# First transfers of a kernel: their order, their division, and their landing times in the planner's account

## The chip, the cores and the metric

One Trainium2 chip, one core. The time is the device time of one execution in microseconds (us), the median of several runs. Engines are named as in the profile: PE (matmul), PEld (its weight loads), DVE (VectorE), ACT (ScalarE), POOL (GpSimd), SP (SyncE; here it only issues transfers). "Lnnn" is a line of the kernel before, unless it is said to be of the changed one.

## The reference, cut to what matters

Eight sequences of 128 tokens with 128 channels (float32) go through eight sublayers, each added to the residual x. The change touches only how the first of them gets its data:

```python
x = x + _L0_xattn_ref(_layernorm(x, axis=-1), ctx_1024, ctx_1024, mask, w_q, b_q, w_k, b_k, w_v, b_v, w_o, b_o)
x = x + _L0_ffn_ref(_layernorm(x, axis=-1), ...)      # soft mixture of slots
x = x + _L1_xattn_ref(_layernorm(x, axis=-1), ctx_1024, ...)
x = x + _L1_ffn_ref(_layernorm(x, axis=-1), ...)      # 64 experts, top 3
...                                                   # L2 and L3: attention, 6 + 2 local layers
```

`_L0_xattn_ref` is a cross attention with 16 heads of 8: queries from the normalised x, keys and values from a context of 77 rows per sequence, with an integer mask of 128 x 77 per sequence, then an output projection. So its keys need w_k, b_k and the context; its values w_v, b_v and the context; its queries x, w_q and b_q; its scores the mask; its output w_o and b_o.

## The kernel before, in words

**Two plans.** The kernel's work is recorded as steps (`plan.add`), each with the engines that may take it and an assumed duration in ns, and then put into an order by a list scheduler (`Plan.arranged`): at each moment of its own account, each engine takes the first recorded step whose inputs have come and for whose tiles there is room. The instructions are then issued in exactly that order, engine by engine. There is one plan for the front (L0 attention, L0 ffn, L1 attention, routing, experts) and another for all later layers. Where two engines may take a step (a copy by ACT or DVE, a spreading of keys by POOL or DVE), the account also decides which does. So an assumed time that changes at the start of the front can move any later step of the front, and the engine that takes it. It can't change the order within the second plan.

**The account's transfers.** A transfer is a step of SP. Its assumed duration blocks SP in the account, and what it writes counts as come a further 2000 ns later (`TAIL`). Before the change the durations grow with size: 540 for two sequences of x, 1000 for the context, 1300 for the pack "wa", 500 for half the masks, 880 for four sequences of x, then 600 (col), 2500 (w0), 3800 (row), 6500 (w1).

**Packs.** Small weights are laid side by side on the host (`Pack`). "wa" holds w_q, w_k, w_v, w_o, a head pattern and four biases of L0's attention: 774 columns, 387 KB. It lies in the tile `wide`, with w0 of the L0 ffn behind it. All of `plan_l0_xattn` is recorded with `plan.also = [come["ctxT"], wav]`: every step of it waits, in the account, for the whole context and all of wa. The built instructions wait only for the transfers that they read.

**The first transfers, on SP's one queue, in this order:** x of sequences 0 and 1 (128 KB), context (308 KB), wa (387 KB), x of 2 and 3 (128 KB), two halves of the masks (154 KB each), x of 4 to 7 (256 KB), col (167 KB), w0 (768 KB), row (1056.5 KB), w1 (2048 KB), cst, wg, eight zero fills of a DRAM table, b2, w, and then expert weights (256 KB each) as tiles come free. As built, from the ninth transfer on each also waits for the transfer eight places before it.

**L0's attention** runs in parts of two, two and four sequences (`some`, L1069). For a part: statistics and normalisation of x (L775, L777 on DVE, L768 to L784 on POOL, L792 on ACT or L794 on DVE), keys (matmul at L761, bias at L1077, spreading over heads at L1081), transposes of the normalised x (L754) and their copy (L741 or L743), queries (L761, bias at L1090), the mask as 0 or -1e30 (L1092). Then for each sequence: values (L761, bias at L924), the mask put into four PSUM banks by a matmul with the identity (L843), scores as 16 small matmuls of 32 rows (L847; the profile has two records for a float32 matmul), exponentials (L855), row sums and outputs as small matmuls of 32 columns (L863), division (L868 to L870), projection (L883, L884), addition to x (L1099).

**The end of the front.** When x is done for the last sequence, its tokens are routed: 24 indirect stores by POOL (L1323), twelve of them behind the last sequences, then reads of the gathered rows by SP (L1381) and the experts (L1421, L1442), whose remaining 90 weight loads stand behind these reads in SP's order.

Of the kernel before, what the change touches and what calls it, by code (L numbers as in the profile page):

```python
# [16 lines left out]
I32 = mybir.dt.int32  # L17
# [7 lines left out]
P = 128  # L25
B = 8
KC = 77
# [38 lines left out]
def gated_bias(b):  # L66

    return padded_rows_halves(b).reshape(6, P).T
# [67 lines left out]
def laid_out(i):  # L136

    i = {k: np.asarray(v) for k, v in i.items()}
    cst = shape_constants()

    row = Pack()
    for name in ("L1_xattn_b_out", "L1_xattn_gate", "L1_ffn_gate_b",
                 "L2_xattn_bv", "L2_xattn_bo", "L2_xattn_g1",
                 "L2_xattn_b1", "L2_xattn_bf2", "L2_xattn_g2", "L2_xattn_b2", "L2_ffn_q_scale",
                 "L2_ffn_k_scale", "L3_ffn_q_scale", "L3_ffn_k_scale"):
        row.add(name, i[name].reshape(1, -1))

# [12 lines left out]
    col.add("L1_ffn_b1", i["L1_ffn_b1"].reshape(NE, 4, P).transpose(2, 0, 1))  # L160

    wa = Pack()
    for name in ("w_q", "w_k", "w_v", "w_o"):
        wa.add("L0_" + name, i["L0_xattn_" + name].T)
    p = np.arange(P)
    wa.add("heads4", (p[:, None] // 8 % 4 == np.arange(4)[None, :]).astype(np.float32))
    for name in ("b_q", "b_k"):
        wa.add("L0_" + name, i["L0_xattn_" + name].reshape(P, 1))
    for name in ("b_v", "b_o"):
        wa.add("L0_" + name, np.broadcast_to(i["L0_xattn_" + name].reshape(1, P), (P, P)))  # L170
# [12 lines left out]
    w = Pack()  # L183
    for n in ("q", "k"):
        w.add(f"L2_W{n}_pair", i["L2_xattn_W" + n][:, np.arange(P) ^ 1])
    for name in ("Wq", "Wk", "Wv", "Wo", "W1"):
        w.add("L2_" + name, i["L2_xattn_" + name])
    w.add("L2_W2", chunked(i["L2_xattn_W2"]))
    w3 = Pack()
    w3.add("L3_q", i["L3_xattn_Wq"])  # L190
    w3.add("L3_kv", i["L3_xattn_Wkv"])
    w3.add("L3_o", chunked(i["L3_xattn_Wo"]))

    def local(m, qkv, wo, a, b):
# [9 lines left out]
    arrays = {  # L204
        "x": i["x"], "mask": i["mask_Bx1xSxS2_if1"].reshape(B, P, KC),
        "maskT": np.ascontiguousarray(i["mask_Bx1xSxS2_if1"].reshape(B, P, KC).transpose(2, 0, 1)),
        "ctxT": np.ascontiguousarray(i["ctx_1024"].reshape(B * KC, P).T),
        "cst": cst.array(), "row": row.array(), "col": col.array(), "wa": wa.array(), "w0": w0.array(), "w1": w1.array(),
        "wg": wg.array(), "w": w.array(), "w3": w3.array(),
        "experts": np.ascontiguousarray(experts), "expert_b2": i["L1_ffn_b2"],  # L210
        "l2a": l2a, "l2b": l2b, "l2o": l2o, "l3a": l3a, "l3b": l3b,
    }
    return arrays, {"cst": cst.at, "row": row.at, "col": col.at, "wa": wa.at, "w0": w0.at, "w1": w1.at, "wg": wg.at,
                    "w": w.at, "w3": w3.at}


# [754 lines left out]
def plan_front(w, early, dram, wide, narrow):  # L971

    c, nc, plan, a = w.c, w.c.nc, w.plan, w.c.a
    c.room("w1", early)

    places = Context.places(plan, wide, narrow)
    n = [a[name].shape[1] for name in ("wa", "w0")]
    c.packs["wa"], c.packs["w0"] = wide[:, 0 : n[0]], wide[:, n[0] : n[0] + n[1]]
    wav, w0v = (plan.part(places[0], lambda t: t) for _ in range(2))
    come = {}  # L980

    def load(name, ns, emit, vals=None):
        come[name] = plan.fixed(None)
        plan.add({"SP": ns}, emit, [], [come[name], *(vals or [])])

    def pack(name, ns):
        load(name, ns, lambda e: c.load(name))

    def x_in(b0, n):
        load("x", 200 + 170 * n, lambda e: nc.sync.dma_start(c.x[:, b0 : b0 + n, :], a["x"][b0 : b0 + n].rearrange("b s d -> s b d")),  # L990
             w.xs[b0 : b0 + n])

    x_in(0, 2)
    load("ctxT", 1000, lambda e: nc.sync.dma_start(c.ctxT, a["ctxT"]))
    plan.add({"SP": 1300}, lambda e: c.load("wa"), [], [wav])
    x_in(2, 2)
    masks = [w.tile([P, 4, KC] if w.general else [KC, 4, P], I32) for _ in range(2)]

    def mask_half(h):
        at = slice(4 * h, 4 * h + 4)  # L1000
        nc.sync.dma_start(masks[h](), a["mask"][at].rearrange("b s k -> s b k") if w.general else a["maskT"][:, at, :])
# [5 lines left out]
    plan.add({"SP": 2500}, lambda e: c.load("w0"), [], [w0v])  # L1007
    pack("row", 3800)
    pack("w1", 6500)
    pack("cst", 3000)  # L1010
# [1 line left out]
    route = Routed(w, early, dram, come)  # L1012
# [25 lines left out]
    plan.also = [w0v, come["col"]]  # L1038
    l0f = plan_l0_ffn(w)
    for part in parts:  # L1040
        l0f(*part)
# [11 lines left out]
            route.some(*then[i])  # L1053
            plan.also = also
    plan.also = [come["col"]]
    route.experts(Context(w, places, (wav, w0v), vzs))
    plan.also = []
    return route


def plan_l0_xattn(w, masks, narrow):
    c, nc, plan = w.c, w.c.nc, w.plan
    wa = lambda name: c.get("wa", name)
# [5 lines left out]
    def some(b0, n):  # L1069
        xs = w.xs[b0 : b0 + n]  # L1070
        xh, xT, qT = w.tile([P, n, P]), w.tile([P, n, P]), w.tile([P, n, P])
        w.normed(lambda k: xh()[:, k, :], lambda k: xs[k](), xs, [xh], n=n)
        mask, fills = masks[b0 // 4], plan.fixed(fill[:, b0 : b0 + n, :])
        ps, kT, kb = w.bank([P, n, KC]), w.tile([P, n, KC]), w.tile([P, n, 4, KC])
        w.mm(lambda: ps().rearrange("p b k -> p (b k)"), lambda: wa("L0_w_k"),
# [3 lines left out]
        def apart(e):  # L1079
# [11 lines left out]
            qT(), qs(), wa("L0_b_q"), float(1.0 / np.sqrt(8.0)), ALU.add, ALU.mult), [qs], [qT])  # L1091
        plan.add({"DVE": 100 + 75 * n}, lambda e: nc.vector.tensor_scalar(  # L1092
            fills(), mask()[:, b0 % 4 : b0 % 4 + n], 0.0, -1e30, ALU.is_equal, ALU.mult), [mask], [fills])
        for j in range(n):
            b, x = b0 + j, xs[j]
            vz = vzs[b % 4]
            w.values_8(b, wa("L0_w_v"), wa("L0_b_v"), vz)
            out = w.attend_8(qT, j, kb, vz, j, wa("L0_w_o"), wa("L0_b_o"), (fills, spread(fill[:, b, :], 4, 1)))
# [1099 lines left out]
```

## Time and profile before

| what | us |
|---|---|
| median of 3 runs | 1552.71 (1550.05 to 1555.53) |
| the profiled execution | 1561.18 |
| its span, first to last instruction | 1559.4 |
| PE busy (share of the span) | 1425.1 (91%) |
| ACT, DVE, POOL busy | 936.9, 920.4, 816.6 |
| mean granted PE clock | 0.952 |

The profiled execution is 8.5 us slower than the median of the others, so a difference is worked out within it and then carried over to the median.

The start of the span, from the timeline of all engines (start and duration in us, engine, line, operation, out<-in, count, and in brackets the idle time before it and what ended it):

```profile
0.72 0.45 SPq L990 DMA_DIRECT2D x_res<-in_x_dram  x1
1.23 0.46 SPq L994 DMA_DIRECT2D ctxT_sb<-in_ctxT_dram  x1
...
1.74 0.42 SPq L256 DMA_DIRECT2D wide<-in_wa_dram  x1
2.21 0.43 SPq L990 DMA_DIRECT2D x_res<-in_x_dram  x1
...
2.95 0.49 DVE L775 BATCH_NORM_STATS2 few<-x_res 128x6 f32<-128x128 f32 x2 [2.95 <-DMA x_res<-in_x_dram]
```

Each issue takes SP about 0.43 us. The first x is issued at 0.72 and DVE starts on it at 2.95.

### The profile page before, as it was taken

How to read it: one execution, taken by the hardware profiler on the slowest of the kernel's cores; microseconds unless marked ns; L12 is line 12 of the kernel's file. 1: busy time of each engine (PE TensorE's matmuls, PEld its weight loads, DVE VectorE, ACT ScalarE, POOL GpSimd, SP SyncE). 2: the span in 40 equal slices, each digit the busy share in tenths (PEclk: the TensorE clock that was granted, in tenths of full speed). 3: DMA queues.
4: the chain of work that ended last, by engine and by line, in shares of the span. 5: the costliest groups of instructions: out<-in, count | busy, mean ns of one | idle time of the engine just before them, and what ended most of it. 6: DMA issues, size and time to landing. Idle time of an engine off the chain costs nothing.

```text
span 1559.4 us, 39024 instructions
## 1 busy us (share of the span) xinstructions
PE 1425.1 (91%) x16007; PEld 972.3 (62%) x16007; DVE 920.4 (59%) x1995; ACT 936.9 (60%) x1917; POOL 816.6 (52%) x1243
## 2 busy tenths in 40 slices
PE   7999998598587869999999999999999999899996
PEld 4777775375363555675666766667666667475654
DVE  5543764523356428668577585766857665657563
ACT  3676564253245846666666666666666676566764
POOL 3310225310566727777595674956749572536561
PEclk7999999699697989999999999999999999999997
DMA  9300001388301000100100010010000000000000
GB/s 335 131 1 21 8 2 42 111 296 324 124 21 69 1 1 1 56 16 2 42 16 15 2 56 16 1 49 23 2 22 22 2 22 2 21 2 1 1 2 16
DMA packets 39964, 74.00 MB, mean 47 GB/s; under 512 B 4102, under 2 KB 18630, under 8 KB 38496
## 3 DMA queue, kind: packets, MB, share of 16 engines
q1 hardware_dynamic: 33888, 66.16, 12.3%
q0 software_dynamic: 1536, 3.15, 0.6%
q8 instruction: 128, 2.10, 0.5%
q10 hardware_dynamic: 4352, 2.10, 0.5%
q14 instruction: 60, 0.49, 0.1%
HBM read 65.10 MB, written 6.29 MB: 46 GB/s over the span
## 4 chain that ended last, share of the span: by engine, by line
PE 59%; DVE 19%; ACT 8%; POOL 7%; issue 4%; DMA 2%; another core or an unknown queue 0%; ACTq 0%; SPq 0%; POOLq 0%; DVEq 0%
PE mm L1757 8%; PE mm L754 7%; PE mm L761 5%; PE mm L1843 5%; DVE big L1779 4%; DVE big L1781 4%; DVE few L1783 4%; PE mm L1868 3%; PE mm L1929 3%; PE mm L1984 3%; PE mm L1961 2%; PE mm L1974 2%; PE mm L863 2%; PE mm L1189 2%; PE mm L1175 2%
## 5 line engine op out<-in xcount | busy, mean ns | idle before, releaser
L741 ACT COPY big<-mm 128x512 f32<-128x512 f32 (+4 forms) x512 | 276.4, 565 | 222.0 <-PE mm L754 118.0
L1784 POOL TENSOR_TENSOR big<-big,big 128x512 f32<-128x512 f32 x224 | 283.8, 1275 | 237.1 <-DVE big L1781 232.0
L1757 PE MATMUL mm<-wide,big 128*128 128x512 f32 x672 | 323.5, 611 | 13.1 <-ACT big L741 10.6
L1797 POOL TENSOR_TENSOR big<-big,few 128x512 f32<-128x512 f32 x224 | 226.8, 1042 | 1.6
L754 PE MATMUL mm<-ident,big 128*128 128x128 f32 (+1 forms) x1430 | 206.4, 280 | 19.5 <-ACT big L792 4.4
L754 PEld LDWEIGHTS mm<-ident,big 128*128 128x128 f32 (+1 forms) x1430 | 162.7, 143 | 96.8 <-POOL big L1797 31.9
L1757 PEld LDWEIGHTS mm<-wide,big 128*128 128x128 f32 x672 | 120.0, 194 | 116.3 <-issue 83.9
L1779 DVE TENSOR_TENSOR big<-mm,big 128x512 f32<-128x512 f32 x224 | 152.4, 680 | 64.0 <-ACT big L1778 61.0
L1778 ACT ACTIVATE big<-mm 128x512 f32<-128x512 f32 x224 | 133.0, 597 | 91.0 <-PE mm L1757 83.5
L1781 DVE TENSOR_TENSOR big<-mm,big 128x512 f32<-128x512 f32 x224 | 152.4, 680 | 5.3 <-ACT big L1778 5.3
L1783 DVE TENSOR_REDUCE few<-big 128x8 f32<-128x512 f32 x224 | 151.0, 674 | 6.5 <-ACT big L1778 6.5
L1875 ACT ACTIVATE big<-mm 128x512 f32<-128x512 f32 x224 | 118.2, 610 | 34.4 <-PE mm L1868 34.4
L1843 PE MATMUL mm<-narrow,big 128*128 128x128 f32 x896 | 117.2, 283 | 11.6 <-DVE big L1891 11.3
L1843 PEld LDWEIGHTS mm<-narrow,big 128*128 128x128 f32 x896 | 108.6, 196 | 28.3 <-DVE big L1891 17.9
L1885 DVE TENSOR_TENSOR mm<-mm,big 128x512 f32<-128x512 f32 x64 | 44.5, 696 | 132.0 <-ACT big L1884 130.5
L1929 PEld LDWEIGHTS mm<-big,big 128*32 128x32 f32 x3072 | 86.7, 110 | 27.9 <-issue 27.2
L1868 PE MATMUL mm<-big,big 64*64 64x64 f32 (+2 forms) x3584 | 100.4, 238 | 1.2 <-ACT big L741 1.2
L1868 PEld LDWEIGHTS mm<-big,big 64*64 64x64 f32 x3584 | 94.2, 133 | 6.3 <-ACT big L741 2.0
L1929 PE MATMUL mm<-big,big 128*32 128x128 f32 x3072 | 94.1, 273 | 0.1
L822 POOL TENSOR_TENSOR big<-big,tiny 128x308 f32<-128x308 f32 x40 | 27.9, 700 | 97.3 <-DVE tiny L819 47.2
L1891 DVE SCALAR_TENSOR_TENSOR big<-mm,big 128x512 f32<-128x512 f32 x112 | 73.1, 686 | 5.6 <-PE mm L1929 0.4
L743 DVE COPY big<-mm 77x512 f32<-77x512 f32 (+2 forms) x74 | 47.6, 656 | 29.7 <-PE mm L1189 9.1
(277 smaller groups left out, 2335.4 us busy)
## 6 DMA issues: line engine op xcount, KB each, us to landing
big<-in_experts_dram SPq DMA_DIRECT2D x128, 256.0 KB, 4.9
wide<-in_l2a_dram SPq DMA_DIRECT2D x6, 1536.0 KB, 6.6
narrow<-in_l2b_dram SPq DMA_DIRECT2D x6, 534.0 KB, 3.5
narrow<-in_l2o_dram SPq DMA_DIRECT2D x6, 512.0 KB, 3.6
p_w<-in_w_dram SPq DMA_DIRECT2D x1, 2048.0 KB
expert_rows<-big SPq DMA_DIRECT2D x8, 256.0 KB, 13.9
big<-expert_rows SPq DMA_DIRECT2D x8, 256.0 KB, 3.8
expert_ys<-big ACTq DMA_DIRECT2D x16, 128.0 KB, 4.3
```

Source lines behind the costliest of these rows:

```text
L741: nc.scalar.copy(out(), in_())
L754: nc.tensor.transpose(tp()[:, k, :], v(k), c.ident)
L1757: self.plan.add({"PE": 860}, lambda e: nc.tensor.matmul(ps(), lhsT=hs()[:, j, :], rhs=wqkv()[:, o : o + 512], start=True, stop=True), [hs, ...
L1778: yield lambda e: nc.scalar.activation(sq(), heads(), AF.Square)
L1779: yield lambda e: nc.vector.tensor_tensor(t1(), heads(), spread(rot()[:, 2 * kind, :], 8, 1), ALU.mult)
L1781: yield lambda e: nc.vector.tensor_tensor(halves(t2()), halves(heads())[:, :, ::-1, :], sin(), ALU.mult)
L1783: yield lambda e: nc.vector.tensor_reduce(ss()[:, lo : lo + 8], sq(), AX.X, ALU.add)
L1784: yield lambda e: nc.gpsimd.tensor_tensor(t1(), t1(), t2(), ALU.add)
L1797: plan.add({"POOL": 1062}, lambda e, t=t, t1=t1, i=i: nc.gpsimd.tensor_tensor(t(), t1(), spread(r()[:, 8 * i : 8 * i + 8], 64, 2), ALU.mul ...
L1843: nc.tensor.matmul(out(), lhsT=oT()[:, k, :], rhs=wo()[:, 4 * g + k, :], start=(g == 0 and k == 0), stop=(4 * g + k == nch - 1))
L1868: nc.tensor.matmul(sc[s]()[at : at + 64, k, q:end], lhsT=kT()[lo : lo + 64, k, at : at + 64], rhs=qT()[lo : lo + 64, k, q:end], start=Fals ...
L1929: nc.tensor.matmul(avs[half]()[32 * t : 32 * t + 32, k, :], lhsT=vs[t // 2]()[:, at : at + 32], rhs=prs[t]()[:, k, :], start=True, stop=True)
```

## The change

The pack wa is divided in two: "wa" keeps w_q, w_k, b_q, b_k and the head pattern (262 columns, 131 KB), and "wb" gets w_v, w_o, b_v, b_o (512 columns, 256 KB). The context is loaded in two halves of 154 KB. The first transfers are recorded in a new order, and their place in the account is new too: each takes SP 470 ns, and comes by the sum of the bytes recorded so far (3.3 ns per KB, plus 2000 ns, less the time that SP has spent, but at least 2000). The steps of L0's attention wait in the account only for their half of the context and for wa, and from the values on for wb as well; the normalisation waits for x alone.

```diff
+    masks = [...]
+    sent = [0, 0]
+
+    def soon(kb, emit, writes):
+        sent[0] += 470
+        sent[1] += kb
+        plan.add({"SP": 470}, emit, [], writes, tail=max(2000.0, 2000.0 + 3.3 * sent[1] - sent[0]))
+
     def x_in(b0, n):
-        load("x", 200 + 170 * n, lambda e: nc.sync.dma_start(...), w.xs[b0 : b0 + n])
+        soon(64 * n, lambda e: nc.sync.dma_start(...), w.xs[b0 : b0 + n])
+
+    def context(h):
+        come["ctxT", h] = plan.fixed(None)
+        at = slice(4 * h * KC, 4 * (h + 1) * KC)
+        soon(154, lambda e: nc.sync.dma_start(c.ctxT[:, at], a["ctxT"][:, at]), [come["ctxT", h]])
...
     x_in(0, 2)
-    load("ctxT", 1000, lambda e: nc.sync.dma_start(c.ctxT, a["ctxT"]))
-    plan.add({"SP": 1300}, lambda e: c.load("wa"), [], [wav])
+    soon(131, lambda e: c.load("wa"), [vals["wa"]])
+    context(0)
+    mask(0)
+    soon(256, lambda e: c.load("wb"), [vals["wb"]])
     x_in(2, 2)
-    for h in range(2):
-        plan.add({"SP": 500}, lambda e, h=h: mask_half(h), [], [masks[h]])
+    context(1)
     x_in(4, 4)
+    mask(1)
     pack("col", 600)
...
-    plan.also = [come["ctxT"], wav]
-    l0x, vzs = plan_l0_xattn(w, masks, places[1])
+    l0x, vzs = plan_l0_xattn(w, masks, places[1], come, vals["wa"], vals["wb"])
     for part in parts:
         l0x(*part)
-    plan.also = []
+        plan.also = []
...
         w.normed(lambda k: xh()[:, k, :], lambda k: xs[k](), xs, [xh], n=n)
+        plan.also = [come["ctxT", b0 // 4], wav]
...
+        plan.also.append(wbv)
         for j in range(n):
             b, x = b0 + j, xs[j]
             vz = vzs[b % 4]
-            w.values_8(b, wa("L0_w_v"), wa("L0_b_v"), vz)
+            w.values_8(b, wb("L0_w_v"), wb("L0_b_v"), vz)
```

What this makes of the built order of instructions:

- **SP**: x 0-1, wa, context 0-3, mask 0-3, x 2-3, context 4-7, x 4-7, wb, mask 4-7, col, w0, row, w1, and the rest as before. wb is recorded fifth but stands eighth, since it lies in the same tile as wa and waits for it in the account. There are two transfers more and the same bytes. 38 expert weights are issued ahead of the reads of the gathered rows, before and after.
- **PE**, first instructions: keys of part 1, of part 2, of part 3 (this one now waits for the second context half), transposes of part 1, three values (the first waits for wb), queries of part 1, the fourth value, then mask, scores, mask, scores. Before: keys, four values, transposes, queries, transposes of part 2, mask, scores, mask, scores. In the four-sequence part the new order has mask and scores of all four ahead of the row sums and outputs of all four.
- **DVE**: both statistics pairs of part 1 now stand ahead of the first key bias. Before, the second pair's aggregation stood behind it.
- **POOL**: one of the three spreadings of keys (616 columns) is now POOL's, ahead of part 2's normalisation.
- The rest of the front up to the routing is listed anew: PE's listed order differs in places up to its row 1,167 of 7,902 and is the same behind it. DVE takes nine normalisations more (L794) and ACT nine fewer (L792).

More of the change, by code (lines that the diff above doesn't have):

```diff
@@ L162, in laid_out @@
     wa = Pack()
-    for name in ("w_q", "w_k", "w_v", "w_o"):
-        wa.add("L0_" + name, i["L0_xattn_" + name].T)
+    wb = Pack()
     p = np.arange(P)
+    for pack, names in ((wa, "qk"), (wb, "vo")):
+        for n in names:
+            pack.add("L0_w_" + n, i["L0_xattn_w_" + n].T)
+    for n in "qk":
+        wa.add("L0_b_" + n, i["L0_xattn_b_" + n].reshape(P, 1))
+    for n in "vo":
+        wb.add("L0_b_" + n, np.broadcast_to(i["L0_xattn_b_" + n].reshape(1, P), (P, P)))
     wa.add("heads4", (p[:, None] // 8 % 4 == np.arange(4)[None, :]).astype(np.float32))
[L167 to L170, printed above, removed]
     w0 = Pack()
@@ L207, in laid_out @@
         "ctxT": np.ascontiguousarray(i["ctx_1024"].reshape(B * KC, P).T),
-        "cst": cst.array(), "row": row.array(), "col": col.array(), "wa": wa.array(), "w0": w0.array(), "w1": w1.array(),
+        "cst": cst.array(), "row": row.array(), "col": col.array(), "wa": wa.array(), "wb": wb.array(), "w0": w0.array(), "w1": w1.array(),
         "wg": wg.array(), "w": w.array(), "w3": w3.array(),
@@ L212, in laid_out @@
     }
-    return arrays, {"cst": cst.at, "row": row.at, "col": col.at, "wa": wa.at, "w0": w0.at, "w1": w1.at, "wg": wg.at,
+    return arrays, {"cst": cst.at, "row": row.at, "col": col.at, "wa": wa.at, "wb": wb.at, "w0": w0.at, "w1": w1.at, "wg": wg.at,
                     "w": w.at, "w3": w3.at}
@@ L976, in plan_front @@
     places = Context.places(plan, wide, narrow)
-    n = [a[name].shape[1] for name in ("wa", "w0")]
-    c.packs["wa"], c.packs["w0"] = wide[:, 0 : n[0]], wide[:, n[0] : n[0] + n[1]]
-    wav, w0v = (plan.part(places[0], lambda t: t) for _ in range(2))
+    lo, vals = 0, {}
+    for name in ("wa", "wb", "w0"):
+        n = a[name].shape[1]
+        c.packs[name], vals[name] = wide[:, lo : lo + n], plan.part(places[0], lambda t: t)
+        lo += n
     come = {}
@@ L987, in pack, with mask @@
         load(name, ns, lambda e: c.load(name))
-    def x_in(b0, n):
-        load("x", 200 + 170 * n, lambda e: nc.sync.dma_start(c.x[:, b0 : b0 + n, :], a["x"][b0 : b0 + n].rearrange("b s d -> s b d")),
-             w.xs[b0 : b0 + n])
+    masks = [w.tile([P, 4, KC] if w.general else [KC, 4, P], I32) for _ in range(2)]
+    sent = [0, 0]
[3 more added lines that the diff above has]
+        plan.add({"SP": 470}, emit, [], writes, tail=max(2000.0, 2000.0 + 3.3 * sent[1] - sent[0]))
+    def x_in(b0, n):
+        soon(64 * n, lambda e: nc.sync.dma_start(c.x[:, b0 : b0 + n, :], a["x"][b0 : b0 + n].rearrange("b s d -> s b d")),
+              w.xs[b0 : b0 + n])
+    def context(h):
+        come["ctxT", h] = plan.fixed(None)
+        at = slice(4 * h * KC, 4 * (h + 1) * KC)
+        soon(154, lambda e: nc.sync.dma_start(c.ctxT[:, at], a["ctxT"][:, at]), [come["ctxT", h]])
+    def mask(h):
+        at = slice(4 * h, 4 * h + 4)
+        soon(154, lambda e: nc.sync.dma_start(
+            masks[h](), a["mask"][at].rearrange("b s k -> s b k") if w.general else a["maskT"][:, at, :]), [masks[h]])
     x_in(0, 2)
-    load("ctxT", 1000, lambda e: nc.sync.dma_start(c.ctxT, a["ctxT"]))
-    plan.add({"SP": 1300}, lambda e: c.load("wa"), [], [wav])
+    soon(131, lambda e: c.load("wa"), [vals["wa"]])
+    context(0)
+    mask(0)
+    soon(256, lambda e: c.load("wb"), [vals["wb"]])
     x_in(2, 2)
[L997 to L1001, printed above, removed]
-    for h in range(2):
-        plan.add({"SP": 500}, lambda e, h=h: mask_half(h), [], [masks[h]])
+    context(1)
     x_in(4, 4)
+    mask(1)
     pack("col", 600)
-    plan.add({"SP": 2500}, lambda e: c.load("w0"), [], [w0v])
+    plan.add({"SP": 2500}, lambda e: c.load("w0"), [], [vals["w0"]])
     pack("row", 3800)
@@ L1037, in plan_front @@
         plan.add({"DVE": 2500}, lambda e: small_scores(c, (("L2_ffn", 6), ("L3_ffn", 2))), [come["row"]], [])
-    plan.also = [w0v, come["col"]]
+    plan.also = [vals["w0"], come["col"]]
     l0f = plan_l0_ffn(w)
@@ L1055, in plan_front, with plan_l0_xattn @@
     plan.also = [come["col"]]
-    route.experts(Context(w, places, (wav, w0v), vzs))
+    route.experts(Context(w, places, vals.values(), vzs))
     plan.also = []
     return route
-def plan_l0_xattn(w, masks, narrow):
+def plan_l0_xattn(w, masks, narrow, come, wav, wbv):
     c, nc, plan = w.c, w.c.nc, w.plan
-    wa = lambda name: c.get("wa", name)
+    wa, wb = (lambda name, pack=pack: c.get(pack, name) for pack in ("wa", "wb"))
     fill = w.once.tile([P, B, KC] if w.general else [KC, B, P], BF16, name="fill")
@@ L1096, in some @@
             vz = vzs[b % 4]
-            w.values_8(b, wa("L0_w_v"), wa("L0_b_v"), vz)
-            out = w.attend_8(qT, j, kb, vz, j, wa("L0_w_o"), wa("L0_b_o"), (fills, spread(fill[:, b, :], 4, 1)))
+            w.values_8(b, wb("L0_w_v"), wb("L0_b_v"), vz)
+            out = w.attend_8(qT, j, kb, vz, j, wb("L0_w_o"), wb("L0_b_o"), (fills, spread(fill[:, b, :], 4, 1)))
             plan.add({"DVE": 282}, lambda e, x=x, out=out: nc.vector.tensor_tensor(x(), x(), out(), ALU.add), [x, out], [x])
```

## The prediction

> **What bounds the kernel now.** I read the chain of waits first: matmuls hold 59% of it, and from 37 to 249 us of the front PE is never idle for a microsecond. So a start that comes earlier is worth its time only if PE then gets through the same work sooner. The opening is another matter. The waits of the first 17.4 us:
>
> ```profile
> PE mm L761 <- DMA wide<-in_wa_dram: 7.3, 1, 7.3
> POOL tiny L768 <- DVE tiny L777: 5.6, 2, 4.8
> DVE big L1077 <- PE mm L761: 4.7, 1, 4.7
> ...
> PE mm L761 <- ACT big L741: 3.6, 1, 3.6
> ```
>
> Columns: who waited for whom, us in total, times, longest. PE's first matmul waits 7.3 us for the pack wa. The other three lines are one knot, and the timeline unties it:
>
> ```profile
> 7.30 2.39 PE L761 MATMUL mm<-ctxT_sb,wide 128*128 128x154 f32 x6 [7.30 <-DMA wide<-in_wa_dram]
> ...
> 8.19 0.38 DVE L1077 TENSOR_SCALAR big<-mm,wide 128x154 f32<-128x154 f32 x1 [4.75 <-PE mm L761]
> 8.48 0.17 DVE L777 BATCH_NORM_AGGREGATE tiny<-few 128x2 f32<-128x6 f32 x1
> ...
> 9.00 0.64 POOL L768 TENSOR_SCALAR tiny<-tiny 128x2 f32<-128x2 f32 x1 [4.77 <-DVE tiny L777]
> ...
> 11.02 0.88 ACT L792 ACTIVATE big<-x_res,tiny,tiny 128x128 f32<-128x128 f32 x2 [9.01 <-DMA wide<-in_w_dram]
> ```
>
> DVE has its statistics by 3.44, but the key bias L1077 stands in its queue ahead of an aggregation, so normalisation, which needs no weight, waits for the weights' transfer. ACT's line names a DMA; the input that came last is POOL's, at 10.98. A copy then stands behind another normalisation on ACT, the query matmul comes at 15.93, and the first mask matmul (L843) at 17.37. From there PE is full, but slow. Busy time (and count) of PE, PEld, DVE, ACT and POOL by stretch, then PE's granted clock, DMA share, GB/s:
>
> ```profile
> 15.00:20.00 5.00, 4.07 (x24) 2.49 (x28) 3.26 (x12) 1.52 (x4) 2.26 (x4) 0.50 0.96 404
> 20.00:25.00 5.00, 5.00 (x61) 3.12 (x53) 3.97 (x12) 2.42 (x5) 2.22 (x4) 0.50 1.07 332
> 25.00:30.00 5.00, 5.00 (x69) 3.62 (x68) 2.26 (x6) 4.92 (x8) 0.35 (x1) 0.50 0.97 280
> 30.00:35.00 5.00, 5.00 (x43) 3.55 (x42) 0.46 (x2) 1.72 (x5) 0.56 (x2) 0.51 1.01 387
> 35.00:40.00 5.00, 5.00 (x110) 3.88 (x109) 2.71 (x7) 1.15 (x4) 0.91 (x2) 1.00 1.05 386
> ```
>
> In half-microsecond stretches the clock falls at 14.42 and is back at 34.90. A group of L843 takes 1.93 us before and 1.06 behind that point, so the slow stretch costs 45% of its PE time.
>
> **The change, step by step.**
>
> *Transfers.* Summing the GB/s of half-microsecond stretches, the bytes ahead of and including wa (842 kB) have moved by 4.95, and wa lands at 7.16; x 4-7 (1551 kB, 8.0) at 3.53+6.5 = 10.0; col (8.6) at 10.5. So a landing trails its bytes by about 2.1 us; only the very first trailed by 0.5. I take the same bytes at the same rates in the new order: context 0-3 (423 kB, 3.5) lands at 5.6, mask 6.1, x 2-3 6.6, context 4-7 (870 kB) 7.15, x 4-7 8.3, wb (1394 kB, 7.4) 9.5. For the first, 4.0 is the other end (a lag of 0.5), and 6.5 if shorter rows move slower.
>
> Here a rule speaks against the change. The Trainium skill, "DMA: Bandwidth & Descriptors", section "Rules for kernel authors", wants many small transfers coalesced into one large one. Were each of the two added transfers to pay the 2.1 us by itself, keys would start at 7.2 + 4.2 − (842−423 kB at about 290 GB/s = 1.4) = 10.0, later than now. But the seven transfers issued from 0.72 to 3.97 overlap their lags in this trace, so two more cost 2 x 0.43 us of SP, which is early. I take the trace.
>
> *Start of PE.* Keys of parts 1 and 2 at 5.6 (1.16 us, from 7.30 to 8.46). Keys of part 3 wait for the context until 7.2 (1.02). Normalisation is no longer behind L1077: aggregations by 3.9, POOL from 4.3 (its fills end at 4.24), its 1.98 us to 6.3, ACT to 7.2, transposes behind the keys 8.2 to 9.0. Three values wait for wb until 9.5 and take 3 x 0.43; the queries, queued behind them though they need only wa, 10.8 to 12.0; a value to 12.4. DVE reaches the bf16 identity for the mask matmul at about 11.9: key biases 0.37, 0.37, 0.52, fills 2 x 0.28, spreadings 0.77 and 1.42, and statistics, the part-3 pair released by PE at 8.3. POOL's spreading costs about 1.4 us (two rows of half its size at 0.70) and delays only part 2's normalisation, due at 16. So the first mask matmul comes at 12.4 instead of 17.37: 5.0 us. Part 2's transposes (0.6) are now behind it: **4.4 us**.
>
> *The clock.* The trace shows no such start, so it is bounded. All changes of the clock that I looked up lie on a grid of 3.413 us (14.42 + 6, 86, 120 and 139 of them give 34.90, 307.94, 424.02, 488.87). The Trainium skill, "TensorE: Matmul & The Clock Gate", Part 1, has the same free-running window, and says a sustained busy one opens the clock. By that rule the full PE from 17.83 should be fast at 21.25. The trace disagrees: windows filled by mask, scores and L863 stay slow until 34.90. Those that open it hold full-size matmuls: 7.59-11.01 (keys and values, full), 31.49-34.90 (scores 2.0 and full ones 1.4). One with 1.6 us of full ones and 0.5 of mask doesn't. In the new order any window inside 5.6 to 12.4 holds 2.5 to 3.0 us of full matmuls, between the two. If one opens the clock and PE goes straight on, it stays open, as from 35 to 60 with the same mixture. At best the 17.5 us of slow work from 17.37 to 34.90 shrink by 45%, **7.9 us**; at worst the slow stretch runs from 12.4 until the first scores and projections stand together, at about 36, and is 23.6 us long: 6.1 us more, 2.7 us lost. Nearest is the window at 7.59, so I take the best.
>
> *What is late next.* With a fast PE, DVE's queue shows: behind queries and fills it has four score checks (3.9 us, L2001 to L2006), then two divisions with 0.95 us reciprocals each. From the copy of part 2's transposes at about 17, checks, query bias, clamps and reciprocals add up so that part 1's outputs come at about 25, where a fast PE alone would need them at 22. I charge **3.0 us**.
>
> *wb's wait.* Behind the first value on PE stand queries, mask and scores; each us of wb beyond 9.5 delays PE by one, until 15 at no loss against before. *Account and fewer waits* cost no instruction. *Nine normalisations from ACT (0.49) to DVE (0.34)*: 3.1 us of DVE time spread over 230 us in which DVE is about half busy; uncovered, 3.1.
>
> *The order up to the routing.* PE's work is the same; idle PE before 223 is under 2 us, so little can be won. In the tail (223 to 272) it idles about 11 us, between L938, softmaxes and POOL's indirect stores. It could change by −4 to +5; the list ends alike (same stores, divisions, 38 weight loads), so I take 0. From the last store all follows in order: gathered rows at 299.57, 90 weight loads behind them on SP, then the unchanged plan; what the routing gains is kept.
>
> Sum: 4.4 + 7.9 − 3.0 = **9.3 us**. From 1561.18 that leaves 1551.9; carried to the median, 1552.71 − 9.3 = 1543.4.
>
> **Rivals.**
>
> *A: the clock opens late in this phase.* If the new start isn't dense enough but scores of sequence 2 with part 2's transposes open it at 21, the work left up to part 1's projections is two pairs of L863 (4.0), mask and scores (2.1), queries, value and projections (2.0), fast: it ends at about 30. Before, it ends at 34.90 + 2.4 (one L863 pair, value and projection, less transposes done early) = 37.3. So 7 us, **1545.7**. For: such a window (2.0 scores, 0.45 full, 0.95 L863) opened it at 424.02. Against: phase decides.
>
> *B: it opens only at about 36.* Then 4.4 − 2.7 = 1.7 us, **1551.0**. For: scores and masks kept it closed for 17 us. Same result if the transfers land late, for example wb at 13.
>
> *C, slower: the tail is listed worse.* One more group of L949 and projection (1.0 + 1.1) with about 2.5 us of key and query matmuls now stands behind the last block of L938. If that block, which lost 7 us between 246 and 254 to issue gaps beside POOL's stores, loses them again and the added 4.6 no longer fits the tail's idle time (4.1 us from 260 to 280), routing is 4.6 later; with a division pushed behind POOL's twelve stores (15.2 us) a few more. It decides once it exceeds B's gain: 1.7 − 4.6 − 4 = −6.9: **1559.6**. Against: one division fewer stands behind the stores, not more.
>
> *D: it doesn't reach PE.* If keys still started at 7.3, normalisation would still gain 4 us, so this falls into B.
>
> **How the numbers follow.** Forecast (about 9 us) 0.50, A 0.17, B 0.22, C 0.11. A measurement here can tell about 0.3%, 4.7 us, from nothing. Forecast: with ±3 us for the relisting 0.90 of it is faster; A 0.75, B 0.15 (0.75 same, 0.1 slower), C all slower. Faster 0.45 + 0.13 + 0.03, and a little for a slow stretch that is longer in other runs of the old kernel: 0.64. Slower 0.11 + 0.02 = 0.13; same 0.23. Low end: 9.3 + 3 from uncharged DVE delay + 3 from the tail: 1537. High end: B and a little of C, 1554.
>
> **What would show it.** Right: first L761 at 5 to 6.5, first L843 at 12 to 13, clock at 1.00 before 15 and kept through 40, gathered rows near 290. Wrong: PE waiting for wb beyond 11 (transfers), half clock from 15 to 30 (A, B), or L843 early and rows at 299 (C). The forecast fails most easily by the clock.

## The result, and the profile after

| | median (us) | runs | range |
|---|---|---|---|
| before, on the same chip | 1560.57 | 20 | 1550.05 to 1567.24 |
| after | 1551.45 | 20 | 1540.53 to 1558.87 |
| ratio | 0.9944 | | 95% interval 0.9924 to 0.9964 |

The ratio is worth 8.7 us (5.6 to 11.9). The kernel before was itself 7.9 us slower here than in the three runs shown ahead of the prediction; both kernels spread over 17 to 18 us from one execution to the next. The profiled execution of the changed kernel took 1547.99 us (span 1546.1, mean clock 0.958), 13.2 less than that of before.

In the changed kernel's profile line numbers have moved: L756, L763, L845, L849, L865 are L754, L761, L843, L847, L863 of before; L940 is L938, L1096 is L1077, L1343 is L1323, L1401 is L1381.

Waits of the first 17.4 us of after (who for whom, us in total, times, longest):

```profile
PE mm L763 <- DMA ctxT_sb<-in_ctxT_dram: 6.3, 2, 5.1
...
ACT big L794 <- POOL tiny L786: 5.6, 2, 3.8
...
DVE big L1096 <- PE mm L763: 3.2, 2, 2.4
```

PE first waits for the context, no longer for wa; ACT waits for POOL's part of the normalisation and not behind it for anything else; VectorE's longest wait for the keys is 2.4 us instead of 4.7. The knot is undone, as the timeline of all engines shows (start, duration, engine, line, and the wait before it):

```profile
3.27 0.30 DVE L779 BATCH_NORM_AGGREGATE tiny<-few 128x2 f32<-128x6 f32 x2
4.33 0.19 POOL L770 TENSOR_SCALAR tiny<-tiny 128x2 f32<-128x2 f32 x1
...
5.12 1.37 PE L763 MATMUL mm<-ctxT_sb,wide 128*128 128x154 f32 x4 [5.12 <-DMA ctxT_sb<-in_ctxT_dram]
...
5.83 0.88 ACT L794 ACTIVATE big<-x_res,tiny,tiny 128x128 f32<-128x128 f32 x2 [3.82 <-POOL tiny L786]
...
9.57 1.56 PE L763 MATMUL mm<-wide,ctxT_sb 128*77 128x128 f32 x6
...
10.92 0.68 PE L763 MATMUL mm<-big,wide 128*128 128x256 f32 x2
...
11.66 1.03 PE L845 MATMUL mm<-fill,identb 77*77 77x512 bf16 x4
```

Both aggregations stand together at 3.27, normalisation runs at 5.83 instead of 11.02, and the first four mask records come at 11.66 instead of 17.37, in 1.03 us instead of 1.91. The stretches of after (busy time of PE, PEld, DVE, ACT, POOL, then granted clock, DMA share, GB/s):

```profile
15.00:20.00 5.00, 5.00 (x142) 4.22 (x138) 4.17 (x13) 4.98 (x10) 2.33 (x4) 1.00 0.98 408
20.00:25.00 5.00, 4.72 (x75) 3.20 (x68) 4.66 (x14) 3.04 (x6) 1.82 (x4) 1.00 1.07 349
25.00:30.00 5.00, 4.99 (x140) 4.20 (x142) 3.66 (x12) 2.54 (x6) 1.36 (x5) 1.00 1.09 301
30.00:35.00 5.00, 5.00 (x74) 3.72 (x66) 4.62 (x14) 0.00 (x0) 1.81 (x4) 1.00 0.99 374
```

The column to read is the clock, 1.00 where before had 0.50, but with one caution: in every profile here it starts at 1.00 and shows the granted clock only from its first recorded change on, and in after that is a fall at 260. Ahead of it the durations tell: a group of four mask records of 1.03 to 1.06 us is fast, one of 1.91 to 1.93 slow. In after all groups from 11.66 to 40 us are fast (one spans 1.20).

What is left of it at the end of the front, from SP's timeline, before and then after (reads of the gathered rows; second load of the last layers' weights l2a):

```profile
299.57 5.25 SPq L1381 DMA_DIRECT2D big<-expert_rows  x8
...
470.61 0.33 SPq L1717 DMA_DIRECT2D wide<-in_l2a_dram  x1
```

```profile
282.28 5.05 SPq L1401 DMA_DIRECT2D big<-expert_rows  x8
...
456.47 0.33 SPq L1737 DMA_DIRECT2D wide<-in_l2a_dram  x1
```

17.3 us are gained at the rows, 14.1 at l2a, 13.3 at the end. So the profile shows more than the sum of the prediction, and half as much again as the medians. The experiments had to settle which of the two parts of the change gains, by which mechanism, and why executions differ so.

### The profile page after: what moved, and what is told of

The parts are those of the page before. It is cut to its first block, busy times and chain, and to the rows that moved or that the text cites. A ratio compares the mean times of both kernels' runs of the same rounds, so it can differ in the third digit from the quotient of the medians.

```text
span 1546.1 us, 39059 instructions
## 1 busy us (share of the span) xinstructions
PE 1416.7 (92%) x16007; PEld 966.6 (63%) x16007; DVE 922.9 (60%) x2008; ACT 932.3 (60%) x1903; POOL 817.9 (53%) x1244
## 4 chain that ended last, share of the span: by engine, by line
PE 58%; DVE 19%; POOL 9%; ACT 7%; issue 4%; DMA 2%; SPq 0%; POOLq 0%; DVEq 0%; ACTq 0%
PE mm L1777 8%; PE mm L756 7%; PE mm L763 5%; PE mm L1863 5%; DVE big L1799 4%; DVE big L1801 4%; DVE few L1803 4%; PE mm L1888 3%; PE mm L1949 3%; PE mm L2004 3%; PE mm L1981 2%; PE mm L1994 2%; PE mm L1209 2%; PE mm L1195 2%; POOL big L1817 2%
## 5 line engine op out<-in xcount | busy, mean ns | idle before, releaser
L743 ACT COPY big<-mm 128x512 f32<-128x512 f32 (+4 forms) x503 | 272.6, 568 | 218.3 <-PE mm L756 116.7
L1777 PE MATMUL mm<-wide,big 128*128 128x512 f32 x672 | 323.7, 611 | 13.2 <-ACT big L743 10.6
L756 PE MATMUL mm<-ident,big 128*128 128x128 f32 (+1 forms) x1430 | 205.3, 280 | 23.6 <-DVE big L745 4.4
L756 PEld LDWEIGHTS mm<-ident,big 128*128 128x128 f32 (+1 forms) x1430 | 162.2, 143 | 99.9 <-POOL big L1817 32.6
L745 DVE COPY big<-mm 128x512 f32<-128x512 f32 (+3 forms) x83 | 51.2, 635 | 29.5 <-PE mm L1209 7.2
## 6 DMA issues: line engine op xcount, KB each, us to landing
p_w<-in_w_dram SPq DMA_DIRECT2D x1, 2048.0 KB, 13.6
```

Source lines behind the costliest of these rows:

```text
L743: nc.scalar.copy(out(), in_())
L756: nc.tensor.transpose(tp()[:, k, :], v(k), c.ident)
L1777: self.plan.add({"PE": 860}, lambda e: nc.tensor.matmul(ps(), lhsT=hs()[:, j, :], rhs=wqkv()[:, o : o + 512], start=True, stop=True), [hs, ...
```

## The experiments

The table is the key to all of them: for each profiled execution, where PE's clock became fast and stayed so, the first indirect store, start and length of the block of 128 small matmuls (L938, or its line in the other kernel) in the middle of the stores, the reads of the gathered rows, the second load of l2a, and the span. All in us.

| kernel | clock fast from | first store | block at, long | rows | l2a | span |
|---|---|---|---|---|---|---|
| before, first profile | 34.9 | 236.4 | 246.0, 11.0 | 299.6 | 470.6 | 1559.4 |
| e1, before again | 25 | 231.2 | 240.7, 11.1 | 296.3 | 474.1 | 1563.4 |
| e9, before, third | 32.8 | 235.0 | 244.5, 2.5 | 296.1 | 474.2 | 1564.2 |
| e3, new transfers alone | 25 to 28 | 232.9 | 242.5, 10.9 | 297.8 | 470.5 | 1558.3 |
| e5, before, busy start | by 16 | 227.6 | 237.2, 2.5 | 288.1 | 460.6 | 1551.4 |
| after, first profile | 11 | 225.7 | 232.4, 2.4 | 282.3 | 456.5 | 1546.1 |
| e2, after again | 13.9 | 227.7 | 234.4, 13.1 | 292.6 | 468.7 | 1556.6 |
| e8, after, third | 10 | 225.8 | 232.5, 2.4 | 282.4 | 458.1 | 1547.4 |
| e10, after, fourth | 11.8 | 225.8 | 232.5, 2.4 | 282.9 | 454.8 | 1542.9 |
| e4, new list alone | by 10.6; slow again 48 to 58 | 230.9 | 237.6, 13.1 | 297.4 | 472.2 | 1562.0 |
| e6, after, busy start | by 11; slow again 50 to 57 | 229.3 | 236.0, 2.4 | 286.0 | 457.8 | 1545.5 |
| e7, new list alone, busy start | 33.9 (fast to 13.2, then slow) | 233.4 | 240.1, 2.4 | 289.9 | 459.3 | 1547.0 |

What comes behind the l2a column takes 1088 to 1091 us in all twelve: everything that differs, differs before it.

**Theory 1** was that the list (the account of landing times) makes the gain, by an earlier mask part and a clock that is open ahead of it, and that the divided and reordered transfers by themselves gain nothing. The rival was that the transfers gain, by bringing the keys' data earlier.

### Each kernel again (e1, e2)

No edit: the kernel before and the kernel after under new names.

> The kernel before, profiled a second time. Every theory: ratio 1.00 within 0.3%. Theory 1 (the opening's slow clock is a property of its order): PE idles between the key/value matmuls and the query matmul again, the first mask matmul (L843) comes at 17 to 17.5 us and the granted clock is 0.50 for at least 14 us after it. Theory 2 (the slow stretch and the 7 us of issue gaps at 246 us were accidents of one execution): no slow stretch of more than 7 us before 60 us, no gaps. Of the gaps alone I expect that they may or may not return; if they do not, about 6 of the 17.3 us by which the gathered rows came earlier in the changed kernel's profile are not the change's.

> The changed kernel, profiled a second time. Theory 1: ratio to the kernel before 0.992 to 0.997; first mask matmul at 11.5 to 12.5 us, clock 1.00 from before 15 us on and kept. Rival (the clock opens in some executions only): half clock at some time between 15 and 30 us in this profile, with the gathered rows read later than in the first profile of this kernel (282.3 us) by 5 us or more.

Measured, with 75 runs of before beside them (median 1562.9): e1 1565.59, ratio 1.0027 (1.0012 to 1.0041); e2 1557.78, ratio 0.9964 (0.9946 to 0.9983). An unchanged kernel under another name thus came out 0.27% off; differences of that size between two kernels of this case are not to be built on. Against e1 instead of the 75 runs, e2's ratio is 0.9950. In e1 the clock was open ten us earlier than in the first profile of before, without any edit (about 9 us of half speed behind the first mask matmul, where at least 14 were expected), and its first matmul began at 5.70 instead of 7.30. Both of the prediction's starting points were late cases of what an execution of the old kernel does.

### The two halves of the change (e3, e4)

e3 has the new transfers in their new order, with the old assumed times:

```diff
-    load("ctxT", 1000, lambda e: nc.sync.dma_start(c.ctxT, a["ctxT"]))
-    plan.add({"SP": 1300}, lambda e: c.load("wa"), [], [wav])
-    x_in(2, 2)
...
+    load("ctxT", 1000, lambda e: (c.load("wa"), ctx_of(0)))
+    plan.add({"SP": 1300}, lambda e: mask_half(0), [], [wav])
+    x_in(2, 2, lambda e: x_of(2, 2))
...
-    for h in range(2):
-        plan.add({"SP": 500}, lambda e, h=h: mask_half(h), [], [masks[h]])
-    x_in(4, 4)
+    plan.add({"SP": 500}, lambda e: ctx_of(1), [], [masks[0]])
+    plan.add({"SP": 500}, lambda e: x_of(4, 4), [], [masks[1]])
+    x_in(4, 4, lambda e: (c.load("wb"), mask_half(1)))
```

> The divided and reordered transfers of the changed kernel, with the order of every other instruction as before (the account is left as it was). Theory 1 (what counts is the order of the instructions, above all the normalisation no longer standing behind the keys, and a PE without a pause): keys at about 5.1 us, but values wait for wb until 9.6, and the query matmul still stands behind ACT's second normalisation: first mask matmul at 16.5 to 18 us, half clock afterwards, ratio 0.998 to 1.003. Rival (the earlier landing of the keys' data is the gain): ratio 0.993 to 0.996, first mask matmul at 15 us or before.

e4 has the new account, and so the new list, with the old transfers in their old order; wa and wb come in one piece:

```diff
-    soon(131, lambda e: c.load("wa"), [vals["wa"]])
-    context(0)
-    mask(0)
-    soon(256, lambda e: c.load("wb"), [vals["wb"]])
...
+    soon(131, lambda e: nc.sync.dma_start(c.ctxT, a["ctxT"]), [vals["wa"]])
+    soon(154, lambda e: c.load("wab"), [come["ctxT", 0]])
+    soon(154, lambda e: x_of(2, 2), [masks[0]])
+    soon(256, lambda e: None, [vals["wb"]])
...
```

> The changed kernel's order of instructions, with the transfers in one piece and in the order of before. Theory 1: keys at 7.3 us as before, then PE without a pause through keys, transposes, values and queries, so that a window of full matmuls opens the clock in every execution; first mask matmul at 12.5 to 14 us, clock 1.00 from before 16 us on; ratio 0.991 to 0.997, as good as the whole change within 0.2%. Rival (the earlier landing is the gain): first mask matmul at 15 us or later, ratio 0.998 to 1.001.

Measured: e3 1563.32, ratio 1.0004 (0.9986 to 1.0022). e4 1559.62, ratio 0.9969 (0.9952 to 0.9986), level with the whole change in the same comparison (0.9964). PE's timeline of e3:

```profile
5.44 1.37 PE L763 MATMUL mm<-ctxT_sb,wide 128*128 128x154 f32 x4 [5.44 <-DMA ctxT_sb<-in_ctxT_dram]
...
16.12 1.22 PE L763 MATMUL mm<-big,wide 128*128 128x256 f32 x2 [4.11 <-ACT big L743]
...
17.56 1.91 PE L845 MATMUL mm<-fill,identb 77*77 77x512 bf16 x4
```

The keys come at 5.44, and nothing follows from it: the queries still wait 4.11 us for a copy that stands behind another normalisation on ACT, and the mask starts at 17.56, slow. And of e4:

```profile
5.65 2.39 PE L763 MATMUL mm<-ctxT_sb,wide 128*128 128x154 f32 x6 [5.65 <-DMA wide<-in_wab_dram]
...
9.54 1.02 PE L763 MATMUL mm<-big,wide 128*128 128x256 f32 x2
...
10.62 0.81 PE L845 MATMUL mm<-fill,identb 77*77 77x512 bf16 x3
```

With the undivided pack the mask is reached at 10.62, no later than with the divided one, since no value waits for wb. So the gain is the list's, and this settles the first question for Theory 1. The divided transfers bring the keys from between 5.6 and 7.3 (undivided: 7.30, 5.70, 6.12, 5.65) to between 4.9 and 5.4 (divided: 4.90 to 5.12 in four profiles of after, 5.44 in e3), and wb's later landing takes up to 1.0 us of it back.

### The clock by itself (e5), and a start that is busier still (e6, e7, e8)

e5 is the kernel before with matmuls on a tile of ones ahead of part 1's keys (16), transposes (9) and queries (17), in banks that are overwritten next. e6 is the kernel after, e7 the kernel e4, with 9 and 3 of them ahead of the keys of parts 1 and 3. e8 is the kernel after again.

```diff
+    def warm(out, n):
+        for _ in range(n):
+            nc.tensor.matmul(out, lhsT=c.ones, rhs=c.ones, start=True, stop=True)
...
+            keep(flat[:, 0:P], {0: 9, 2: 0, 4: 3}[b0])
+            nc.tensor.matmul(flat, lhsT=wa("L0_w_k"), rhs=c.ctxT[:, b0 * KC : (b0 + n) * KC], start=True, stop=True)
```

> The kernel before, with nothing moved: 16 extra 128x128 f32 matmuls on a tile of ones stand ahead of part 1's first keys, 9 ahead of its transposes and 17 ahead of its queries, each written into the PSUM bank that the step fills next, so that TensorE is busy from about 5 us on. Theory 1 (a large part of the gain is the clock that opens before the mask part): the mask matmuls take 1.03 to 1.06 us a row of four from the first on, at about 16 to 18 us, instead of 1.9; in the two profiles of this kernel the slow stretch ran from 15.8 to about 25 us in one and from 17.4 to 34.9 in the other, at half speed 4.6 to 8.8 us, less up to 3 us that VectorE's queue takes back, so 3 to 5 us less than before: ratio 0.997 to 0.998. Theory 2 (the gain of the list is its order, with the queries no longer behind a wait of 3.5 us; the clock is covered by VectorE): 0 to 1 us, ratio 0.9995 to 1.0005, and VectorE shows longer stretches of busy time between 16 and 40 us.

> The kernel after, with 9 extra 128x128 f32 matmuls on ones ahead of part 1's keys and 3 ahead of part 3's keys. Theory 1: the clock opened at about 10.5 and 13 us in the two profiles of after without them, in some executions surely later; with them it is open at the first keys or before the mask part in all, worth 0.5 to 1 us where it opened early anyway and up to 3 where not: 1 us below after on the mean (range 0 to 2.5), ratio to before about 0.995. Theory 2: no difference from after within 1 us, since what follows waits for VectorE. Slower than after by more than 1 us would mean that the extra work delays the keys.

> The new account and list with the old undivided transfers, as in the run with the list alone, and the same 9 and 3 extra matmuls. If the divided transfers add nothing but an earlier stretch of busy TensorE, this is level with the run above within 1 us (ratio about 0.996). If they bring the keys and values forward in a way that lasts to the end, this stays 1 to 2 us behind it.

> The kernel after once more, beside the three above on one chip, so that they have their own base. From the two comparisons so far (0.9944 and 0.9964): 0.9955, between 0.994 and 0.997. In its profile the clock opens before 14 us; the gathered rows start between 282 and 293 us as in the other two, by where the clock closes after 239 us.

Measured, beside 33 runs of before (1560.48):

| | median | runs | ratio (95%) |
|---|---|---|---|
| e5 | 1558.28 | 22 | 0.9985 (0.9968 to 1.0002) |
| e6 | 1549.75 | 6 | 0.9914 (0.9885 to 0.9943) |
| e7 | 1550.15 | 12 | 0.9925 (0.9900 to 0.9950) |
| e8 | 1547.09 | 6 | 0.9907 (0.9878 to 0.9937) |

PE's timeline of e5 shows the old order with a fast clock (L1106 and L1099 are its queries and transposes):

```profile
15.46 0.60 PE L1106 MATMUL mm<-big,wide 128*128 128x256 f32 x2
15.90 0.38 PE L1099 MATMUL mm<-ident,big 128*128 128x128 f32 x2
16.12 1.03 PE L843 MATMUL mm<-fill,identb 77*77 77x512 bf16 x4
```

The mask part begins where it did in e9 (16.07) and its first store comes at 227.6 instead of 235.0: **7.3 us for the clock alone** up to that store, with nothing moved, in one execution of each (the two ran on different chips). In the new list the same difference can be read between e7 (slow from 13.2 to 33.9) and e8: 233.4 against 225.8, 7.5 us.

The medians show less of it, 2.3 us with an interval that holds zero, and between what the two theories expected. Two things would account for a part: in other executions of the old kernel the clock opens earlier by itself (e1, e3), and later stretches of slow clock give some of it back (e7 is 7.5 us behind e8 at the rows and 1.3 at l2a). But e5 and e8 were measured together and both start with a fast clock, and still their medians are 11.2 us apart, where their profiles are 4.0 apart; e5's profiled execution is among its fastest (1553.24, median 1558.28). So the profiles show what the clock is worth at the front of one execution. How the gain of the medians divides between the clock and the order of the list is not shown.

In e7 the start was filled and the clock closed all the same. PE reached the mask at 9.50 and then waited for VectorE:

```profile
9.50 1.04 PE L845 MATMUL mm<-fill,identb 77*77 77x512 bf16 x3
12.13 0.38 PE L845 MATMUL mm<-fill,identb 77*77 77x512 bf16 x1 [1.59 <-DVE big L1114]
```

The 3.41 us up to the change at 13.2 (one step of the prediction's grid of clock changes) hold only 1.75 us of PE's work.

e8 came out lower than it was expected to (0.9955, no lower than 0.994), which the next section takes up. e6, e7 and e8 don't differ beyond their intervals: filling the start further gains nothing that these runs can tell, and in e6 the clock, open ahead of the first mask matmul, closed again at 50. The undivided transfers under the new list (e7) are again level with the divided ones. None of the versions tried here beat the changed kernel.

### Why the ratios differ: the block between the stores (e9 to e12)

The changed kernel's ratio was 0.9944, 0.9964 and 0.9907 in three comparisons. In all four profiles of the comparison that gave 0.9964 the block of 128 small matmuls took 11 to 13 us, as in the first profile of before; in none of the four of the comparison that gave 0.9907. PE's timeline of e2, part of it:

```profile
234.43 0.94 PE L940 MATMUL mm<-big,big 64*64 64x77 f32 x41
236.38 0.35 PE L940 MATMUL mm<-big,big 64*64 64x77 f32 x4 [1.01 <-issue]
237.80 0.36 PE L940 MATMUL mm<-big,big 64*64 64x77 f32 x3 [1.07 <-issue]
...
244.91 2.63 PE L940 MATMUL mm<-big,big 64*64 64x77 f32 x70 [0.42 <-issue]
```

and of after, with the same instructions in the same order:

```profile
232.41 2.44 PE L940 MATMUL mm<-big,big 64*64 64x77 f32 x128
```

In e2 PE gets through 41 records, then through one to four at a time, idle in between with nothing that the profile could name, until 244.91. POOL's last indirect store of this group runs from 241.89 to 242.85, so the full pace comes back 2.06 us behind its end. In the other four stalled profiles it does so 2.05 to 2.15 us behind it (before: 253.71, last store until 251.56), so the end of the stall goes with the end of the stores. In e2 the clock also closes, from 239.1 to 249. The DMA view of 226 to 246 lists two instruction queues in after:

```profile
q0 software_dynamic: 384, 0.79, 11.5%
q8 instruction: 1, 0.02, 0.3%
q14 instruction: 2, 0.02, 0.3%
```

(packets, MB, share), and in e2 the stores' queue alone:

```profile
q0 software_dynamic: 384, 0.79, 11.4%
```

That would fit an instruction stream that isn't refilled while the stores move. Not every stalled profile bears it out, though. In e4 both queues are silent during the stall as well, but in before, e1 and e3 each moves one packet in it. The DMA view of before, 246 to 253.7, lists among others:

```profile
q8 instruction: 1, 0.02, 0.8%
q14 instruction: 1, 0.01, 0.4%
```

So the missing packets are not what the five stalls have in common. To test whether the stores cause them, e11 and e12 are the kernels before and after without the indirect stores (the experts then read zeros); e9 and e10 are both kernels again, as their base.

```diff
-                def put(e, j=j, k=k):
-                    ...
-                    put = nc.gpsimd.indirect_dma_start(
-                        out=self.rows[:, :], out_offset=bass.IndirectOffsetOnAxis(ap=dsti[:, j, k : k + 1], axis=0),
-                        in_=xh()[:, j, :], in_offset=None)
+                def put(e):
+                    pass
```

> The kernel before once more, as the base of this chip: ratio 1.000, within 0.997 to 1.003. Its profile says whether this chip stalls TensorE in the block of 128 small matmuls that follows the first indirect stores: in six of ten profiles so far the block took 9 to 13 us instead of 2.4, with TensorE idle and waiting for nothing that the profile shows. With the stall the gathered rows are loaded 53 to 56 us after the block's start, without it about 51.

> The kernel after once more. Theory 1 (the block begins about 10 us earlier in every execution, and the stall, where it comes, costs this list about 9 us and the old list about 4): ratio 0.996 to 0.997 if this chip stalls in both profiles, 0.991 to 0.993 if it stalls in neither; in between if the executions are mixed. Block start 232 to 235 us, against 240 to 246 in before. Theory 2 (the ratios of the three comparisons differ by chance alone): 0.994 to 0.995 whatever the stall.

> The kernel before without its indirect stores of the chosen rows: the experts then compute on the zeros that the start writes; every other instruction stays, in the same order. Theory 1 (the stall comes from those stores: [...]the packets of the instruction queues are missing from the trace as long as the stall lasts): the block of 128 small matmuls takes 2.4 to 2.5 us with no idle row in it, also if the kernel before stalls on this chip, and the rows are loaded 5 us earlier or more, as the wait for the stores goes too. Rival (the stall belongs to TensorE's own instruction stream at that place): the block takes 9 us or more here too, whenever it does in the run of before.

> The kernel after without the same stores. Theory 1: no stall, the block takes 2.4 to 2.5 us and begins at 231 to 235 us, about 10 us ahead of the run above; what the change is worth with no stall in either is then 8 to 12 us between this run and the one above, a ratio of the two of 0.992 to 0.995. Rival: the block is as long as in the run of after on this chip.

Measured, beside 35 runs of before (1560.16): e9 1561.91, ratio 1.0006 (0.9983 to 1.0029); e10 1548.55, 0.9932 (0.9912 to 0.9953); e11 1551.56, 0.9941 (0.9916 to 0.9966); e12 1537.97 in four runs, 0.9855 (0.9812 to 0.9899).

By the table five of the ten profiles before these four had stalled, not six, as e9's expectation counts. Neither e9 nor e10 stalls (2.5 and 2.4 us), so that the unstalled blocks of e11 and e12 (2.4 us each, at 244.5 and 241.9) say nothing about the stores: **on the cause of the stall this test is inconclusive**, and it stays open. What did come out is close to what e10's expectation said for no stall, a ratio between 0.991 and 0.993. With the stall the change was worth 0.36%, without it 0.68% and 0.93%, and 0.56% where the first profile of before stalled and that of after did not. Only e2's and e8's intervals lie apart; that of e10 holds the 0.994 of the rival too. Each of the three later comparisons also ran on a chip of its own, one execution of each kernel was profiled in it, and against e1 the 0.36% are 0.50%. So this is an ordering that fits, not a proof. The rows of the table say by how much: from the first store to the rows it is 63.2 to 65.1 us with the stall in the old list and 60.5 and 61.1 without; in the new list 64.8 and 66.5 with it, 56.6 to 57.1 without.

The medians of e12 and e11 lie 13.6 us apart, more than the 8 to 12 expected. But e12 gave one more answer. Its block came at 241.9, not at 231 to 235: the clock did not open at the start. PE's timeline of e12:

```profile
11.28 0.63 PE L763 MATMUL mm<-wide,ctxT_sb 128*77 128x128 f32 x2
11.71 1.91 PE L845 MATMUL mm<-fill,identb 77*77 77x512 bf16 x4
13.55 2.01 PE L849 MATMUL mm<-big,huge 32*77 32x128 f32 x32
```

In this execution the clock became fast at about 35 only. That is the prediction's rival B, in one of the five profiles of the new list with the new transfers and no added matmuls. e11's clock opened at 33.5, so the two show what the list does at a slow clock: the block comes 2.6 us earlier, the first read of the gathered rows 3.9 (262.2 against 266.1). The l2a load, however, comes 13.1 us earlier (454.8 against 468.0). What makes the other nine us between the rows and l2a is open. Changes of the clock on the grid of 3.413 us, counted back from the first recorded one, give the windows of the start; PE's busy time in them, in e10 and then in e12:

```profile
8.35:11.76 3.41, 3.09 (x14) 2.41 (x12) 2.38 (x5) 0.37 (x1) 3.16 (x5) 1.00 1.04 386
```

```profile
8.36:11.78 3.42, 2.81 (x12) 2.42 (x12) 2.54 (x5) 0.37 (x1) 3.17 (x5) 1.00 1.00 371
```

With 3.09 us of 3.41 the clock opened at the window's end, with 2.81 it didn't. The other profiles fit: after with 3.35 and e8 with 3.18 opened, e2 with 2.40 (PE waited 1.0 us for wb in it) opened a window later. Two windows of the old list, worked out in the same way, fit too: 2.9 in e9 and 3.4 in e11 opened. So for full-size matmuls the turning point of these profiles lies between 2.8 and 2.9 us of 3.41, and 0.3 us of PE work in one window decide over 7 us.

## Why the prediction was right

The forecast (9.3 us, 1543.4 from the base then known) stands against 8.7 us (5.6 to 11.9) measured; the time, 1551.45, lies in the range, 8 us above the forecast because the base was 7.9 us higher. That the two gains are so close is partly luck: the later comparisons gave 5.6, 14.5 and 10.6 us, and two terms erred in opposite directions, the clock, worked out from the latest opening seen with the old list, and the tail, put at nothing where it is 4 us shorter without the stall. By its own steps:

- **Transfers.** Keys were put at 5.6 with 4.0 as the other end: 5.12, and 4.90 to 5.09 in four other profiles. wb was put at 9.5: PE begins the values at 9.57, and at 9.47, 9.14 and 9.07 where the wait shows. The working by which each added transfer pays its own lag, with the keys at 10.0, was rightly set aside for the overlapping lags. The rule behind it hardly bears on this case: the Trainium skill, "DMA: Bandwidth & Descriptors", section "Rules for kernel authors", calls transfers under 64 KB mostly overhead, and the divided ones here have 131 to 256 KB; no run has smaller ones in their place. The step overrated what the transfers matter: the 7.3 us of the old profile were a late case, and e3 and e4 show that the transfers gain nothing by themselves.
- **Start of PE, 4.4 us.** First mask matmul at 11.66 instead of the predicted 12.4. With e5 and e10, both at a fast clock, it is 16.12 against 11.76, 4.4.
- **The clock, 7.9 us at best.** The best case came in four of the five profiles of the new list with the new transfers: 7.3 (e5 against e9) and 7.5 (e8 against e7) at the first store. That the clock then stays open, if PE goes straight on, is not refuted: it closed in e4, e6 and e7, with gaps of 1.2 to 1.6 us. "Between the two" was the right reading of a window with 2.5 to 3.0 us of full-size matmuls: it opened with 3.09 and stayed shut with 2.81. The rule of a sustained busy window in the Trainium skill, "TensorE: Matmul & The Clock Gate", Part 1, was rightly not taken alone for the old start: e9's PE is busy from 16.07 on without a gap and its clock opens at 32.8. For the new start, where the busy window holds full-size matmuls, rule and trace agree.
- **What is late next, 3.0 us.** The size was near, the place was not. At a fast clock the mask starts 4.4 us earlier and the first store only 1.8 (227.6 against 225.8), so 2.6 were lost. But PE doesn't wait for VectorE's checks of part 1: between 12 and 35 us of after it idles for 0.3 us. The waits are late, in the part that was said to have little in it either way ("idle PE before 223 is under 2 us"). From the waits of after up to 226 us:

```profile
PE mm L756 <- DVE tiny L821: 1.3, 1, 1.3
PE mm L756 <- POOL big L824: 1.2, 2, 1.1
PE mm L1307 <- POOL before L1300: 0.7, 1, 0.7
```

  The first two, at 160 to 211 us, are reciprocals and divisions of softmaxes that the transposes wait for. e5 has neither; from the first mask matmul to the first store PE idles 1.85 us in it, and 5.05 in after. This is read from the two lists side by side and was not tried apart.
- **The tail, 0 between −4 and +5.** Without the stall it is 4 us shorter (56.6 to 57.1 from store to rows, against 60.5 and 61.1), of which 2.9 lie ahead of the block, which begins 6.7 us behind the first store instead of 9.6; with it about 1 us longer. The sum to the first store, 4.4 + 7.3 − 2.6 = 9.1, met the predicted 9.3 where the clock opened late before and early after; the rows of the profile, 17.3 earlier, hold the tail besides, a stall that only the old kernel's profile had, and a late start of that profile. "Rows near 290" was therefore 8 us off in this execution, and about right for e2 (292.6). About 3 of the 17.3 us were given back by 471, as the l2a lines show.
- **Rival C** named the stalled block as a danger to the new list. It is one: with a stall the new list loses 8 to 10 us from store to rows, the old one 2 to 5. But it doesn't outweigh the start.

## What to carry to other kernels

When a list scheduler works from assumed landing times, correct the assumed times before dividing the transfers: here the account gave the gain and the transfers alone none that could be told. A clock that opens by the work of one short window can make a start of dense full-size matmuls worth more than the idle time it removes (up to 7.3 us to the first store here), and a gap of a few tenths can lose it, so compare several profiles of the same kernel before believing one. Where executions of one kernel spread over 1%, read gains at milestones (first store, rows, a fixed load) and between profiles in the same condition. Don't take a gain at a milestone for one at the end: between the rows and l2a alone the three profiles of the old kernel took 171.0, 177.9 and 178.2 us.

## What was not expected of the hardware

- One gap of little more than a microsecond can be enough for the clock to close. In e4, row sums and outputs (L865, 32 columns each) with one gap of 1.23 us at 45.7 were followed by half speed from 48 to 58 although PE was busy again; e6, with a gap of 1.40 us at 48.6, did the same from 50 to 56.5, and e7 closed behind its 1.59 us at 10.5. The windows that ended with these changes held 2.18, 2.23 and 1.75 us of PE's work. Whether the small matmuls in them count for less was not tried.
- A block of 128 small matmuls took 2.4 us or 11 to 13 us with the same instructions, in all four profiles of one comparison and in none of the next six that had the stores. The cause is open. The only lead is the end of the stall, 2.05 to 2.15 us behind the last indirect store in all five; the stores alone don't bring it about, since they stand beside the block in the fast cases too.
- The same transfer (wa, third in the old order) let PE start at 5.60, 5.70, 6.12 or 7.30.
